# Cross-attention with an image prompt: each group's second pair of probability transfers issued by ScalarE instead of SyncE

## The chip, the core and the metric

The kernel runs on one core of a Trainium2 chip. A core has TensorE (PE, matrix products), VectorE (DVE), ScalarE (ACT), GpSimd (POOL) and SyncE (SP), each with its own instruction stream, and 16 DMA engines that move data between on-chip memory (SBUF) and device memory (HBM), and within SBUF. An engine works its instructions in the order of its stream; it waits for the others by semaphores. A transfer is an instruction in the stream of the engine that issues it; the profile shows these rows as SPq for SyncE's queue and ACTq for ScalarE's. The metric is the device time of one execution in microseconds, lower is better.

## The reference

Eight sequences (B = 8) of 112 rows and 320 channels attend to a context of 375 rows of 512 numbers, of which the last 4 are image-prompt tokens. There are 20 heads of 16 channels.

```python
q = heads(hidden_states @ W_q)
k_t = heads(text_ehs @ W_k)                    # 371 text rows
v_t = heads(text_ehs @ W_v)
probs_t = softmax(einsum('bhsd,bhtd->bhst', q, k_t) * attn_scale)
text_out = einsum('bhst,bhtd->bhsd', probs_t, v_t)
k_ip = heads(ip_ehs @ W_k_ip)                  # 4 prompt rows
v_ip = heads(ip_ehs @ W_v_ip)
attn_scores = einsum('bhsd,bhnd->bhsn', q, k_ip) * attn_scale
qsem = l2norm(einsum('bhst,bte->bhse', probs_t, text_ehs))
sem = einsum('bhse,bne->bhsn', qsem, l2norm(ip_ehs))
probs_ip = softmax(attn_scores + 0.5 * sem) * spatial_mask
ip_out = einsum('bhsn,bhnd->bhsd', probs_ip, v_ip)
out = (text_out + ip_out) @ W_out + b_out + hidden_states
```

The norm of `qsem` is computed through the Gram matrix of the context (p G p instead of the length of p times the context), so that one product of the probabilities with a table that holds the Gram matrix, the prompt's columns and the values gives everything that follows.

## The kernel before, in words

**Tiling.** The 20 heads of a batch are five groups of four. A step is one pair (b, g) of batch and group, 40 in all; the loop at L1246 works the first 35, and the last batch's five steps are written out behind it. The four heads a = 0 to 3 of a group sit in the four quadrants of 32 rows of PE.

**What a step does for its own group.** `multiplied(b, g)` (L781) sets off 48 products of the transposed probabilities `xgT` with the group's table `u` into four PSUM banks `ps_qd`, one for each head. `value_sums` (L794, ACT) copies the value columns out, `reduced` (L827, DVE) multiplies the Gram part with the probabilities and sums it; after these two the banks are free for the next step.

**What a step does for groups to come.** The scores of the group two steps ahead (LEAD = 2) are made in two pairs. `ahead(n)` names them: `now`, heads 2 and 3 of that group, at the step's start, and `then`, heads 0 and 1, of which the scores are made late in the products and the probabilities behind them. (`more` is empty but in the last two steps of the loop, where it brings in pairs of the last batch.) For a head, `scores` (L719) makes the PSUM tile `ps_s`, `probabilities` takes the maximum on DVE (L742), the exponential on ACT (L745) and, from batch 1 on, copies the four prompt logits on ACT (L747). Then `sent` (L754) moves the 112 x 371 probabilities, 162.3 KB, into the tile `xg` of a ring, 32 partitions for each head. One step before they are used, DVE transposes all of `xg` to `xgT` (L762, `transposed`), for which all four heads must have landed.

**What else stands in the queues.** SP issues nearly all transfers, in the order of the program: beside L754 the Gram tables to the groups (`u<-ug`, L553), the values to device memory and back (`vd<-vext`, L627; `vr<-vd`, L636; POOL copies them into `u` at L688), the next contexts (`ct`, L160 and L165), the next inputs (`xr_sb`, L127; `x_sb`, L1212) and the results. ACT also copies PSUM to SBUF: keys `kT` (L573 and L584), values `vext` (L618), the attention result `aT` (L987), and in the loop's last step two banks of products to `shared` (L812) for a sum that POOL and ACT take over from DVE. Between the products of two steps PE makes keys (L568, L577), values (L611), queries (L377), Gram blocks (L535) and the output of the batch before (L983, L995).

**PSUM.** `ps_qd` has four banks, `ps_sc` two for scores, `ps_mm` two for everything else. From batch 2 to 6 the last chunk of a batch's keys (L568), and the result L983 in some batches, take one of the two score banks ("spare"); the copy by ACT (L573, L987) frees it for the next scores.

**Order.** PE, SP, DVE and ACT run in the order in which the source is written (a manual schedule; POOL's is left to the scheduler within the loop). In the loop the `then` probabilities come behind `value_sums` and ahead of `reduced`, `placed` and the loads; in ACT's stream the copies of keys, values and `aT` of the stretch between two steps follow them.

Of the kernel before, what the change touches and what calls it, by code (L numbers as in the profile page):

```python
# [20 lines left out]
def kernel(  # L21
# [14 lines left out]
    nc = tc.nc  # L36
    P = 128
    B, S, C = x.shape
# [3 lines left out]
    TT = T - NIP  # L42
# [8 lines left out]
    RG = 32  # L51
# [11 lines left out]
    QN = P // RG  # L63
# [21 lines left out]
    def bank(name, spare=False):  # L85

        if spare:
            return ps_sc.tile([P, 512], F32, tag="sc", name=name)
        return ps_mm.tile([P, 512], F32, tag="mm", name=name)
# [304 lines left out]
    st = {}  # L394
# [115 lines left out]
    def gram_banks(b):  # L510

        st["ps_g", b] = ps = [bank(f"ps_g_{b}_{c}") for c in range(2)]
        for n, t in enumerate(ps):
            cleared(t, n + 1)
# [34 lines left out]
    def gram_to_groups(b, blocks, eng=nc.sync, parts=range(GROUP)):  # L549

        for q in blocks:
            for a in parts:
                eng.dma_start(  # L553
                    st[b]["u"][a * RG : (a + 1) * RG, q * GW : (q + 1) * GW],
                    ug[q * RG : (q + 1) * RG, :],
                )
# [152 lines left out]
    def scores(b, g, a, early=False, ps=None):  # L709
        s = st[b]  # L710
        _, qm, j = queries[b]
        i, r = g // 2, g % 2
        if early and (g + a // 2) % 2:

            ps = ps_qd.tile([P, 512], F32, tag="qd", name=f"ps_s_{b}_{g}_{a}")
        elif ps is None:
            ps = ps_sc.tile([P, 512], F32, tag="sc", name=f"ps_s_{b}_{g}_{a}")
        w = T if b > 0 else TT
        nc.tensor.matmul(  # L719
            ps[:S, :w],  # L720
            qm[a * RG : (a + 1) * RG, i, r, j * S : (j + 1) * S],
            s["kT"][a * RG : (a + 1) * RG, i, :w],
            start=True,
            stop=True,
        )
        s["sc", g, a] = ps

    def home(b, g):

        if b == B - 1 and g == 1:  # L730
            t = io.tile([P, NT, E], F32, tag="ct", name=f"p_{b}_{g}").rearrange("p c e -> p (c e)")
        elif b == B - 1 and g == 3:
            t = wv_sb.rearrange("p e f -> p (e f)")
        else:
            return work.tile([S, GROUP, TT], F32, tag="p", name=f"p_{b}_{g}", bufs=3)
        return t[:S, : GROUP * TT].rearrange("p (a t) -> p a t", t=TT)

    def probabilities(b, g, a, hold=False):
        s = st[b]
        ps = s.pop(("sc", g, a))  # L740
        nmx = small.tile([S, 1], F32, tag="nmx", name=f"nmx_{b}_{g}_{a}", bufs=4)
        nc.vector.tensor_reduce(nmx, ps[:S, :TT], AX.X, ALU.max, negate=True)  # L742
        if ("p", g) not in s:
            s["p", g] = home(b, g)
        nc.scalar.activation(s["p", g][:, a, :], ps[:S, :TT], AF.Exp, bias=nmx)  # L745
        if b > 0:
            nc.scalar.copy(s["ipl"][:, groups[g][a], :], ps[:S, TT:T])  # L747
        if not hold:
            sent(b, g, a)

    def sent(b, g, a):

        xg = x_ring[(b * NG + g) % NX]
        nc.sync.dma_start(xg[a * RG : a * RG + S // QN, :, :TT], st[b]["p", g][:, a, :])  # L754

    def transposed(b, g):

        xg = x_ring[(b * NG + g) % NX]
        xT = work.tile([P, BLK, P], F32, tag="xgT", name=f"xgT_{b}_{g}")
        n = BLK // 2 if b == B - 1 else BLK  # L760
        for j in range(0, BLK, n):
            nc.vector.transpose(  # L762
                xT[:, j : j + n].rearrange("p j (k q) -> p q j k", q=QN),
                xg[:, :, j * RG : (j + n) * RG].rearrange("p q (j k) -> p q j k", k=RG),
            )
        st[b]["xT", g] = xT

    def multiplied(b, g):
        s = st[b]
        xT = s.pop(("xT", g))  # L770
        banks = []
        for a in range(GROUP):

            if b == B - 1 and g % 2:
                banks.append(bank(f"ps_qd_{b}_{g}_{a}", spare=a > 1))
            else:
                banks.append(ps_qd.tile([P, 512], F32, tag="qd", name=f"ps_qd_{b}_{g}_{a}"))
        for j in range(BLK):
            c, q = PLACE[j] if b > 0 else (j // QN, j % QN)
            for a in range(GROUP):  # L780
                nc.tensor.matmul(  # L781
                    banks[a][:S, j * RG : UW],
                    xT[a * RG : (a + 1) * RG, j, :S],
                    region(b, c)[a * RG : (a + 1) * RG, q, j * RG - c * P :],
                    start=(j == 0),
                    stop=(j == BLK - 1),
                )
            yield
        s["qd", g] = banks
# [315 lines left out]
    def run(key, make, pieces=1):  # L1105

        if key not in gens:
            gens[key] = make()
        for _ in range(pieces):
            next(gens[key], None)  # L1110
# [123 lines left out]
    def ahead(n):  # L1234

        c, d = steps[n + LEAD : n + LEAD + 2]
        if steps[n] == (B - 2, NG - 2):
            todo = ((c, 2, 3), (c, 0, 1), (d, 2, 3))
        elif steps[n] == (B - 2, NG - 1):
            todo = ((c, 0, 1), (d, 2, 3), (d, 0, 1))  # L1240
        else:
            todo = ((c, 2, 3), (c,), (c, 0, 1))
        return [[(t[0], a) for a in t[1:]] for t in todo]

    ctx.enter_context(tc.manual_schedule(engines=engines | {mybir.EngineType.Activation}))
    for n, (b, g) in enumerate(steps[:-NG]):  # L1246
        now, more, then = ahead(n)
        late = (b, g) == (0, NG - 2)
        for c, a in now if not late else ():
            scores(*c, a)  # L1250
            probabilities(*c, a)
        for j, _ in enumerate(multiplied(b, g)):
            if j == 0:
                for c, a in now if late else ():
                    scores(*c, a)
                    probabilities(*c, a)
                for c, a in more:
                    scores(*c, a, ps=bank(f"ps_s_{c[0]}_{c[1]}_{a}"))
                    probabilities(*c, a, hold=True)
            if j == 6:  # L1260
                for c, a in then:
                    scores(*c, a)
            if j == 2:
                if g == 0:
                    gram_banks(b + 1)
                transposed(*steps[n + 1])
                for c, a in more:
                    sent(*c, a)
                if 1 <= g <= 3:
                    gram_to_groups(b + 1, {1: (0,), 2: (1,), 3: (3,)}[g], parts=halves[g == 2])  # L1270
                for c, i in x_loads.get((b, g), ())[: int(n > 0)]:
                    load_x_blocks(c, i)

                if g in (1, 2) and b > 0:
                    run(("f", b - 1), None)
        value_sums(b, g)
        if g == 2 and b > 0:
            run(("f", b - 1), None)
        if n == NG - 1:
            run(("t", b), lambda: prompt_logits(b))  # L1280
        for c, a in then:
            probabilities(*c, a)
        if n == len(steps) - NG - 1:
            sums = shared(b, g, GROUP // 2)
            next(sums)
            reduced(b, g, 2)
        else:
            reduced(b, g)
        placed(*steps[n + 1])
        if g == 0 and b > 1:  # L1290
            run(("f", b - 2), None)
        load_rest(n)
        if n == 0:
            load_next(2)
        if g in ctx_blocks and b < B - 3:
            load_ctx_blocks(b + 3, ctx_blocks[g])
        for c, i in x_loads.get((b, g), ())[1:]:
            load_x_blocks(c, i)
        if g == 1:
            gram_to_groups(b + 1, (0,), parts=halves[1])  # L1300
            gram_to_groups(b + 1, (1,), parts=halves[0])
        elif g == 2:
            gram_to_groups(b + 1, (2,))
        elif g == 3:
            gram_to_groups(b + 1, (3,), parts=halves[1])
            values_to_groups(b + 1)
        if g in (2, 3) and b == 0:
            run(("pp",), None)
        if (b, g) == (B - 2, 0):
            prompt_values_by_head()  # L1310
        if (b, g) == (B - 2, 1):
            bd = load_prompt_values_by_head()
        if g == 0 and b > 0:
            prompt_values(b - 1)
        between(b, g)
        if g == 1:
            values_to_dram(b + 1, nc.sync, 0, 2)
        if g == 2:
            values_to_dram(b + 1, nc.sync, 2)
# [10 lines left out]
    b = B - 1  # L1330
# [126 lines left out]
```

## Time and profile before

| what | value |
|---|---|
| median of 3 runs | 427.07 us (423.07 to 427.16) |
| the profiled execution | 426.04 us, span 424.3 us, granted clock 0.999 |
| PE busy | 415.8 us, 98% of the span |
| DVE busy | 331.5 us, 78% |
| ACT busy | 185.5 us, 44% |
| POOL busy | 111.2 us, 26% |
| DMA traffic | 65.84 MB, mean 155 GB/s |

The span is the time from the first to the last instruction that the profile records. The shares are means over the span; the digits of a slice on the page (not shown) are the same in tenths. DMA issues do not count as busy, so that SP has no share. A timeline row gives the start in us, the duration, the engine, the line, the operation with output and inputs, the number of like instructions in a row, and in brackets how long the engine sat idle ahead of it and what ended that. A scores row with "x2" is one pair of heads side by side.

### The profile page before, as it was taken

To read this page: it belongs to the slowest core of one execution; us is meant where nothing else is said; L and a number is where in the kernel's file an instruction comes from. 1 tells how busy PE (TensorE), PEld (TensorE's weight loads), DVE (VectorE), ACT (ScalarE), POOL (GpSimd) and SP (SyncE) were. 2 spreads that over 40 slices of the span, in tenths; PEclk is the share of its full clock that TensorE was granted. 3 is DMA by queue.
4 is the path that set the end of the run, shared out by engine and by line. 5 is a ranking of instruction groups with operands and counts; after the bars stand their busy time and mean duration, and the time that the engine had idled before them with its cause. 6 is when DMAs were issued, how large, how long until landed. Compare 5 with 4: busy or idle time off the path is not lost.

```text
span 424.3 us, 14021 instructions
## 1 busy us (share of the span) xinstructions
PE 415.8 (98%) x5500; PEld 327.3 (77%) x5500; DVE 331.5 (78%) x693; ACT 185.5 (44%) x647; POOL 111.2 (26%) x277
## 2 busy tenths in 40 slices
PE   8999999999998999999999999999999999999995
PEld 8867767878776977779778887788778887787993
DVE  5037668869896987889789987987898986888873
ACT  2344332335333463334533463333634363446773
POOL 6411100011160120602133220602124120515550
PEclk9999999999999999999999999999999999999999
DMA  8676846565766565666656556655555556465200
GB/s 256 184 191 198 187 122 181 155 174 152 192 157 169 141 170 154 158 175 175 169 142 167 144 158 164 159 145 158 167 151 151 134 162 181 135 167 166 66 2 29
DMA packets 61687, 65.84 MB, mean 155 GB/s; under 512 B 22072, under 2 KB 55648, under 8 KB 61622
## 3 DMA queue, kind: packets, MB, share of 16 engines
q1 hardware_dynamic: 60990, 63.98, 56.5%
q8 instruction: 44, 0.72, 0.8%
q10 hardware_dynamic: 632, 0.96, 0.7%
q14 instruction: 21, 0.17, 0.1%
HBM read 20.23 MB, written 5.32 MB: 60 GB/s over the span
## 4 chain that ended last, share of the span: by engine, by line
PE 83%; DVE 4%; ACT 3%; DMA 3%; issue 3%; SPq 2%; POOL 0%; DVEq 0%; POOLq 0%
PE ps_qd L781 34%; PE ps_v L611 14%; PE ps_k L577 10%; PE ps_s L719 9%; PE ps_g L535 7%; DMA xg<-p 2%; PE ps_q L377 2%; PE ps_o L995 2%; PE ps_g L491 1%; DVE xgT L762 1%; DVE nmx L742 1%; ACT shared L820 1%; SPq L553 1%; PE ps_w L467 1%; SPq L636 1%
## 5 line engine op out<-in xcount | busy, mean ns | idle before, releaser
L781 PE MATMUL ps_qd<-u,xgT 32*112 32x360 f32 (+11 forms) x3840 | 219.5, 351 | 1.2 <-POOL u L688 1.2
L781 PEld LDWEIGHTS ps_qd<-u,xgT 32*112 32x112 f32 x3840 | 189.1, 172 | 27.0 <-POOL u L688 2.4
L762 DVE STREAM_TRANSPOSE xgT<-xg 128x1536 f32<-128x1536 f32 (+1 forms) x45 | 119.7, 2680 | 13.9 <-DMA xg<-p 9.4
L745 ACT ACTIVATE p<-ps_s,nmx 112x371 f32<-112x371 f32 x156 | 84.9, 586 | 61.5 <-DVE nmx L742 49.3
L742 DVE TENSOR_REDUCE nmx<-ps_s 112x1 f32<-112x371 f32 x160 | 76.9, 526 | 28.3 <-PE ps_s L719 27.3
L827 DVE CUSTOM_DVE_ANT_0 junk<-ps_qd,p 112x371 f32<-112x371 f32 x146 | 79.2, 543 | 17.9 <-PE ps_qd L781 1.5
L719 PE MATMUL ps_s<-kT,qm 32*112 32x375 f32 (+1 forms) x320 | 66.7, 497 | 0.0
L688 POOL COPY u<-vr 128x64 f32<-128x64 f32 x120 | 25.7, 236 | 152.5 <-PE ps_qd L781 90.2
L611 PE MATMUL ps_v<-wv_sb,ctxT 128*128 128x384 f32 (+1 forms) x192 | 63.0, 477 | 0.0
L611 PEld LDWEIGHTS ps_v<-wv_sb,ctxT 128*128 128x128 f32 x192 | 35.7, 190 | 20.9
L794 ACT COPY pvs<-ps_qd 112x21 f32<-112x21 f32 x151 | 16.2, 189 | 74.8 <-PE ps_qd L781 74.5
L577 PE MATMUL ps_k<-ctxT,wk_sb 128*128 128x371 f32 x136 | 46.9, 488 | 0.2 <-DVE ctxT L458 0.2
L577 PEld LDWEIGHTS ps_k<-ctxT,wk_sb 128*128 128x128 f32 x136 | 24.4, 189 | 14.0 <-issue 0.5
L719 PEld LDWEIGHTS ps_s<-kT,qm 32*112 32x112 f32 x320 | 23.7, 170 | 12.6 <-issue 10.9
L535 PE MATMUL ps_g<-ctxT 128*32 128x375 f32 (+11 forms) x672 | 30.4, 333 | 0.0
L535 PEld LDWEIGHTS ps_g<-ctxT 128*32 128x32 f32 x672 | 27.7, 110 | 2.0
L618 ACT COPY vext<-ps_v 128x384 f32<-128x384 f32 (+1 forms) x24 | 11.2, 465 | 40.0 <-PE ps_v L611 39.5
L747 ACT COPY ipl<-ps_s 112x4 f32<-112x4 f32 x140 | 24.3, 174 | 0.0
L386 DVE TENSOR_SCALAR qm<-ps_q,emask 128x224 f32<-128x224 f32 (+1 forms) x25 | 9.0, 394 | 17.3 <-PE ps_q L377 17.2
L970 POOL TENSOR_TENSOR wv<-vip,w 112x1280 f32<-112x1280 f32 x6 | 14.8, 2464 | 27.7 <-DVE w L910 27.7
L437 DVE STREAM_TRANSPOSE ctxT<-ct 128x512 f32<-128x512 f32 x18 | 20.0, 1110 | 0.0
L508 POOL TENSOR_TENSOR ug<-ug,half 128x128 f32<-128x128 f32 (+1 forms) x24 | 10.4, 447 | 30.6 <-ACT ug L507 30.6
(174 smaller groups left out, 320.7 us busy)
## 6 DMA issues: line engine op xcount, KB each, us to landing
xg<-p SPq DMA_DIRECT2D x156, 162.3 KB
u<-ug SPq DMA_DIRECT2D x124, 99.0 KB
ct<-in_ctx_dram SPq DMA_DIRECT2D x24, 176.0 KB
vr<-vd SPq DMA_DIRECT2D x32, 120.0 KB
vip<-vipd SPq DMA_DIRECT2D x6, 560.0 KB
vd<-vext SPq DMA_DIRECT2D x7, 320.0 KB
vd<-vext SPq DMA_DIRECT2D x7, 160.0 KB
out_dram<-ob SPq DMA_DIRECT2D x8, 140.0 KB
```

Source lines behind the costliest of these rows:

```text
L437: nc.vector.transpose(ctxT[:, :, c * P : (c + 1) * P].rearrange("p e (j i) -> p j e i", i=RG), ct[:, some, :].rearrange("p j (k e) -> p j ...
L535: nc.tensor.matmul(ps[c][q * RG : (q + 1) * RG, j * RG - c * P : T - c * P], ctxT[:, e, j * RG : (j + 1) * RG], ctxT[:, e, j * RG : T], st ...
L577: nc.tensor.matmul(ps[:, :TT], wk_sb[:, e, i * P : (i + 1) * P], s["ctxT"][:, e, :TT], start=(e == 0), stop=(e == NE - 1),)
L611: nc.tensor.matmul(ps[:, :w], ctxT[:, e, c * P : (c + 1) * P], wv_sb[:, e, :w], start=(e == 0), stop=(e == NE - 1),)
L688: nc.gpsimd.tensor_copy(v, dealt(b, c, s["vr"][:, c * QN : (c + 1) * QN, g, :]))
L719: nc.tensor.matmul(ps[:S, :w], qm[a * RG : (a + 1) * RG, i, r, j * S : (j + 1) * S], s["kT"][a * RG : (a + 1) * RG, i, :w], start=True, st ...
L742: nc.vector.tensor_reduce(nmx, ps[:S, :TT], AX.X, ALU.max, negate=True)
L745: nc.scalar.activation(s["p", g][:, a, :], ps[:S, :TT], AF.Exp, bias=nmx)
L747: nc.scalar.copy(s["ipl"][:, groups[g][a], :], ps[:S, TT:T])
L762: nc.vector.transpose(xT[:, j : j + n].rearrange("p j (k q) -> p q j k", q=QN), xg[:, :, j * RG : (j + n) * RG].rearrange("p q (j k) -> p ...
L781: nc.tensor.matmul(banks[a][:S, j * RG : UW], xT[a * RG : (a + 1) * RG, j, :S], region(b, c)[a * RG : (a + 1) * RG, q, j * RG - c * P :], ...
L827: nc.vector.tensor_tensor_reduce(out=junk, in0=ps[:S, :TT], in1=s["p", g][:, a, :], scale=1.0, scalar=0.0, op0=ALU.mult, op1=ALU.add, accu ...
```

## The change

`sent` gets the issuing engine as an argument. For the `then` pair in the loop, `probabilities` is called with `hold=True`, so that it issues no transfer, for both heads; then both transfers are issued in ScalarE's own stream, behind the exponentials and the prompt copies of both. Before, each transfer was issued on SyncE's queue. The `now` pair, the `more` pairs, the prologue and the last batch keep SyncE.

```diff
         if not hold:
             sent(b, g, a)
 
-    def sent(b, g, a):
+    def sent(b, g, a, eng=nc.sync):
 
         xg = x_ring[(b * NG + g) % NX]
-        nc.sync.dma_start(xg[a * RG : a * RG + S // QN, :, :TT], st[b]["p", g][:, a, :])
+        eng.dma_start(xg[a * RG : a * RG + S // QN, :, :TT], st[b]["p", g][:, a, :])
...
         for c, a in then:
-            probabilities(*c, a)
+            probabilities(*c, a, hold=True)
+        for c, a in then:
+            sent(*c, a, nc.scalar)
         if n == len(steps) - NG - 1:
             sums = shared(b, g, GROUP // 2)
             next(sums)
```

In the built program 70 transfers move from SyncE's queue to ScalarE's, two in each of the 35 steps; the order on PE, DVE and POOL is the same.

## The prediction

> **What bounds the kernel.** I read the page's busy shares and its chain first, then the history of the tile `xg`, then the timelines of single steps.
>
> ```profile
> PE 415.8 (98%) x5500; PEld 327.3 (77%) x5500; DVE 331.5 (78%) x693; ACT 185.5 (44%) x647; POOL 111.2 (26%) x277
> PE 83%; DVE 4%; ACT 3%; DMA 3%; issue 3%; SPq 2%; POOL 0%; DVEq 0%; POOLq 0%
> ...
> L754 SPq DMA_DIRECT2D xg<-p x156: 800/856/1557, 26.9 to 397.8; - x156
> ...
>   DVE xgT L762: 12.1, 8
> ```
>
> TensorE (PE) is busy in 98% of the span and makes 83% of the chain that ends last. The moved transfers are 70 of the 156 rows of L754 (two in each of the 35 steps of the loop), at a median of 0.856 us: 60 us of issue leave SyncE's (SP's) queue. That is no gain by itself: DVE's transposes waited for `xg` for 12.1 us in all, and only where PE waits after them is there anything to win. So I look for the places where PE lost time, and then for those where it will.
>
> In a step PE does the two scores "now", then the value products L781, then other work (keys, values, grams). Without a stall the distance from the first score to that other work is 5.36 us (180.05 to 185.41):
>
> ```profile
> 180.05 0.57 PE L719 MATMUL ps_s<-kT,qm 32*112 32x375 f32 x2
> ...
> 185.41 1.87 PE L995 MATMUL ps_o<-wo_sb,aT 128*112 128x320 f32 x6
> ```
>
> **What the change removes from SP's path.** Three stalls of PE come from late issues on SP, all in batch 1.
>
> ```profile
> 83.28 3.26 SPq L636 DMA_DIRECT2D vr<-vd  x4
> ...
> 87.15 3.66 SPq L754 DMA_DIRECT2D xg<-p  x4
> 88.94 0.58 POOL L688 COPY u<-vr 128x64 f32<-128x64 f32 x3 [7.07 <-DMA vipd<-ipkv]
> 87.19 1.35 PE L719 MATMUL ps_s<-kT,qm 32*112 32x375 f32 x4
> 89.23 3.89 PE L781 MATMUL ps_qd<-u,xgT 32*112 32x392 f32 x54 [0.68 <-POOL u L688]
> 93.53 3.08 DVE L762 STREAM_TRANSPOSE xgT<-xg 128x1536 f32<-128x1536 f32 x1 [2.83 <-DMA xg<-p]
> 94.65 1.77 PE L535 MATMUL ps_g<-ctxT 128*32 128x375 f32 x22
> 98.92 0.57 PE L719 MATMUL ps_s<-kT,qm 32*112 32x375 f32 x2
> 104.99 5.43 PE L611 MATMUL ps_v<-wv_sb,ctxT 128*128 128x384 f32 x16
> ```
>
> - Step (1,0), that is batch 1, group 0: 87.19 to 94.65 is 7.46, so 2.1 lost. PE waited for POOL's copies, which began at 88.94, 2.4 after the issue of `vr` had ended (83.28 + 3.26 = 86.54). Two pairs of transfers fewer lie ahead of `vr` on SP; one alone is worth 2 x 0.856 = 1.7. I take 1.8 of the 2.1.
> - Step (1,1): 98.92 to 104.99 is 6.07, 0.7 lost, after a transpose that waited 2.83 for `xg`. The four sends before it ended at 90.81, and the transpose began 2.72 later: that is also my landing time for this transfer. With the pair on ScalarE (ACT) I take the 0.7 back.
> - Step (1,4):
>
> ```profile
> 127.43 1.56 SPq L553 DMA_DIRECT2D u<-ug  x2
> 129.11 1.84 SPq L754 DMA_DIRECT2D xg<-p  x2
> ...
> 133.88 2.96 DVE L762 STREAM_TRANSPOSE xgT<-xg 128x1536 f32<-128x1536 f32 x1 [2.64 <-issue]
> ...
> 137.88 0.54 PE L568 MATMUL ps_k<-ident,k 128*128 128x128 f32 x3 [1.33 <-ACT ipl L747]
> ```
>
> The pair's issue ended at 130.95, the transpose began 2.93 later, its tail held PE 1.33. SP runs late here, and loses the pair of the step before as well, so that everything comes up to 1.7 earlier; I take 1.1.
>
> Gains: 1.8 + 0.7 + 1.1 = **3.6 us**. Everywhere else the transfers were hidden by PE already. [...]
>
> **What the change puts on ACT.** Each pair now holds ACT's queue behind the second exponential and its copy L747. What is queued behind it: `kT` copies L573/L584, the aT copy L987, `vext` L618, in the last loop step the copies L812, then the next exponentials. The price of an issue by ACT:
>
> ```profile
> L553 ACTq DMA_DIRECT2D u<-ug x4: 598/604/611, 16.8 to 18.7; - x4
> L553 SPq DMA_DIRECT2D u<-ug x5: 589/597/675, 16.3 to 19.0; - x5
> ```
>
> ACT took 604 ns for a `u` where SP took 597 in the same stretch and 588 in the whole run, so I take SP's 0.87 for an `xg` (half of 1.74), 1.74 a pair. The two issued at the same time and neither got longer. [...]
>
> Second, and larger: the built program gives the DMAs of both queues eight completion semaphores in turn, in the order of its listing, and a DMA waits until the one before it on its semaphore has landed. On one queue that one is old. Now ACT's pair can be dealt a semaphore that SP used for a load of the same step, and the wait stands in ACT's queue. From the built program, step by step: nothing costly in most; in these it falls late.
>
> Step (2,4): the pair waits for the two `ct` loads, which SP issues behind what used to follow the pair.
>
> ```profile
> 186.83 1.74 SPq L754 DMA_DIRECT2D xg<-p  x2
> ...
> 189.20 0.92 SPq L160 DMA_DIRECT2D ct<-in_ctx_dram  x2
> ...
> 187.64 0.47 ACT L573 COPY kT<-ps_k 128x371 f32<-128x371 f32 x1 [0.67 <-PE ps_k L568]
> ...
> 188.68 0.57 PE L719 MATMUL ps_s<-kT,qm 32*112 32x375 f32 x2
> ```
>
> Without the pair SP reaches `ct` at 187.46, or 0.8 before that as it was already late; the first has left at 187.1 to 187.9, and lands 2.4 later (the `vr` row's 2.4), about 189.5 to 190.3. Two issues end at 191.2 to 192.0, the `kT` copy 0.5 later, and the second score needs the PSUM bank that this copy frees: at 188.8 before, at 191.7 to 192.5 after. Loss 2.9 to 3.7; I take 2.9, as SP's late start should go.
>
> Step (4,3): the pair waits for two `u` issued just ahead.
>
> ```profile
> 272.77 1.21 SPq L553 DMA_DIRECT2D u<-ug  x2
> ...
> 276.14 0.45 ACT L987 COPY aT<-ps_a 128x336 f32<-128x336 f32 x1
> ...
> 277.11 0.57 PE L719 MATMUL ps_s<-kT,qm 32*112 32x375 f32 x2
> ```
>
> First `u` away at 273.4, landed 275.4 (2.0 later) to 275.8 (2.4); pair until 277.1 to 277.5; `kT` and aT copies until 277.9 to 278.3; the second score needs aT's bank at 277.2: 0.7 to 1.1, taken 0.7. Step (6,3) is alike, with four sends between:
>
> ```profile
> 366.61 4.03 SPq L754 DMA_DIRECT2D xg<-p  x4
> ...
> 372.33 0.45 ACT L987 COPY aT<-ps_a 128x336 f32<-128x336 f32 x1
> ...
> 372.82 0.58 PE L719 MATMUL ps_s<-kT,qm 32*112 32x375 f32 x2
> ```
>
> The pair's first waits for the last of the four, landed between 373.3 (370.64 + 2.7) and 371.4 (if SP, with pairs gone from its queue, is 2 earlier); aT comes 2.6 after that, where the second score stood at 372.8: 1.2 to 3.1, taken 1.2.
>
> Step (6,4), without any wait for a semaphore:
>
> ```profile
> 380.18 0.91 ACT L812 COPY shared<-ps_qd 112x371 f32<-112x371 f32 x2
> ...
> 380.93 1.29 PE L781 MATMUL ps_qd<-u,xgT 32*112 32x392 f32 x10 [0.26 <-POOL u L688]
> ```
>
> The copies that free two banks for the third and fourth of these products move behind 1.74 of issue; they ended at 381.09, and I put PE's need of them at 0.4 after its start: 1.3, between 0.9 and 1.74.
>
> Smaller: (4,4) 0.2 (its `xr` loads land as the pair is ready), the rest of the steps with their copies 0.5. Losses: 2.9 + 0.7 + 1.2 + 1.3 + 0.2 + 0.5 = **6.8 us**.
>
> The pairs themselves lose nothing by landing later: DVE's own wait for `xg`, were it 1 us longer, is covered by PE's keys, values and grams (the 2.83 above cost PE 0.7). SP's later DMAs can wait for a semaphore of ACT's pair too, but of a pair one or more steps old, long landed: 0.
>
> **Sum.** 426.04 (the profiled execution: 424.3 span and 1.74 around it) - 3.6 + 6.8 = 429.2. The median of before is 427.07, 1.03 above that execution, so a median of after should be **430.2**.
>
> **Rivals.**
> - *Only SP's relief counts* (the other side): the semaphores' predecessors land earlier than I work out, since SP, with 60 us less to issue, runs ahead; then (2,4), (4,3), (6,3) cost 1 together and the tail little. For it: SP was behind in batch 1. Against: the `ct` of (2,4) is issued after work that needs that step's exponentials. 427.07 - 3.6 + 1 = 424.5; it decides where `ct` lands before the pair's own exponentials are done (187.0 in (2,4)), and if the early steps with no PE row of mine gain too it goes to 422.
> - *ACT's issues are longer, and every copy behind them is late.* In `xg` groups of four an issue took 4.03 / 4 = 1.0, not 0.87, and the longest was 1.56. Ten steps (all of group 4, the odd batches' group 3) have no slack between copy and second score: at 0.5 more a pair 5 us more, at 1.4 14 more: 435 to 444. It decides when an ACT row of L754 passes 0.9.
> - *Hidden either way:* PE covers both the stalls and the holds; 427.1. [...] For it: PE at 98%. Against: the PSUM banks.
> - *The change does not free the pair from SP*, since its semaphores tie it to SP's loads in 20 or so steps: gains gone but losses there, 427.07 + 6.8 = 433.9.
>
> **How the numbers follow.** Forecast (428 to 433) 0.45; SP's relief 0.18; long issues 0.15; hidden 0.10; tied 0.12. About 1% is what a measurement of this kernel can tell from no change (422.8 to 431.3). Faster: the low end of the relief, 0.08. Slower: the long issues, the tied ones and about a third of the forecast, 0.42. Within: 0.50. The range reaches from the relief's 424 to the near part of the long issues, 437.
>
> **What would show it.** ACT rows of L754, 70 of them, near 0.87; in (2,4) an ACT idle of over 2 us ahead of them, and PE's second score there waiting for L573; PE's wait for POOL at 89.23 and the 1.33 before L568 gone; SP never four `xg` in a row in batch 1; PE's products after the loop's last step waiting for L812. I am wrong if no PE wait of over 1 us stands in (2,4), or if the rows on ACT are above 1 us, or if `kT` copies hold PE in most steps.

## The result

The changed kernel takes 451.24 us (median of 6, 446.58 to 452.69), the kernel before 426.96 beside it: a ratio of 1.0563, 95% interval 1.0494 to 1.0632. It is 24 us slower; the forecast was 3 slower, and the range ended at 437.

The page of the changed kernel: busy time, the granted clock of PE in 40 slices of the span (9 is full), then the DMA queues (packets, MB, share of the 16 engines).

```profile
span 451.0 us, 13942 instructions
...
PE 428.7 (95%) x5500; PEld 337.4 (75%) x5500; DVE 331.9 (74%) x693; ACT 186.5 (41%) x647; POOL 111.6 (25%) x277
...
PEclk9999998989999999998999999999999699999999
...
q1 hardware_dynamic: 52170, 52.34, 45.2%
q10 hardware_dynamic: 9452, 12.60, 10.6%
```

DVE and ACT do the same work in the same time. PE does the same 5500 products, but is busy for 12.9 us longer and idle for 13.8 us longer (451.0 - 428.7 = 22.3, where it was 424.3 - 415.8 = 8.5). Part of why it is busier stands in the row of the granted clock, which has four slices below 9. In the kernel before it had none:

```profile
PEclk9999999999999999999999999999999999999999
```

The bytes moved are in the queue of ACT (q10) as the change says.

The history of the tile `xg`, as it was shown of before:

```profile
L754 SPq DMA_DIRECT2D xg<-p x86: 801/847/1159, 26.8 to 424.4; - x86
L754 ACTq DMA_DIRECT2D xg<-p x70: 819/822/924, 44.3 to 406.4; - x70
...
  DVE xgT L762: 17.6, 9
```

An issue by ACT costs 0.822 us in the median, and one of the 70 passes 0.9, with 0.924. The price of the issue was right, and the rival of long issues is out. What went wrong lies between the issues.

Where the time came in can be read from the start of each step's first product L781 in the two timelines. The difference after less before grows to 26.6 us, in a few places:

| between the starts of steps | grows by (us) | what stands there in the changed kernel |
|---|---|---|
| (0,2) and (0,3) | 6.5 | pairs of (0,1) and (0,2) waiting; half clock |
| (1,0) and (2,0) | 3.5 | half clock from 97.3 on; small stalls |
| (2,4) and (3,1) | 4.0 + 1.8 | pair of (2,4) waiting; half clock |
| (3,4) and (4,0) | 2.4 | pair of (3,3) waits and lands late |
| (5,4) and (6,1) | 3.7 + 1.9 | pair of (5,3) waits and lands late; half clock twice |
| (6,3) and (6,4) | 1.2 | pair of (6,3) waiting |
| (7,0) and (7,1) | 1.5 | copies L812 behind the pair of (6,4) |

The rest adds up to less than 1 us. Three mechanisms make most of these numbers, and each is shown by its rows.

**One: ACT stands in wait.** Step (2,4), timelines of SP, ACT and PE:

```profile
196.55 1.90 SPq L160 DMA_DIRECT2D ct<-in_ctx_dram  x2
...
197.16 0.17 ACT L747 COPY ipl<-ps_s 112x4 f32<-112x4 f32 x1
200.39 1.79 ACTq L754 DMA_DIRECT2D xg<-p  x2
202.22 0.47 ACT L573 COPY kT<-ps_k 128x371 f32<-128x371 f32 x1 [4.89 <-DMA xg<-p]
...
202.74 0.65 PE L719 MATMUL ps_s<-kT,qm 32*112 32x375 f32 x1 [3.04 <-ACT kT L573]
```

The pair's data are ready at 197.3, and ACT issues it at 200.39, after the two `ct` loads of SP that were dealt the same semaphores (106 and 107 in the trace) just before; the `kT` copy waits behind for 4.89, and PE for the copy for 3.04. Step (0,1) is alike, behind a `u` and a `ct` load: its first transfer begins 4.2 us after its exponential has ended. The delay runs on into (0,2); rows of ACT, DVE and PE:

```profile
61.08 1.93 ACTq L754 DMA_DIRECT2D xg<-p  x2
63.05 0.48 ACT L618 COPY vext<-ps_v 128x384 f32<-128x384 f32 x1 [5.74 <-DMA xg<-p]
...
66.45 2.96 DVE L762 STREAM_TRANSPOSE xgT<-xg 128x1536 f32<-128x1536 f32 x1 [4.48 <-DMA xg<-p]
...
71.20 1.83 ACTq L754 DMA_DIRECT2D xg<-p  x2
73.08 0.24 ACT L324 COPY kip<-ps_kip 128x96 f32<-128x96 f32 x1 [2.27 <-DMA xg<-p]
...
73.37 2.61 PE L377 MATMUL ps_q<-xT,wq_sb 128*128 128x224 f32 x6 [3.34 <-ACT kip L324]
```

**Two: the pair lands late, on top of what it waits.** Step (5,3), where the first transfer had stood in wait for 1.59 us behind `u` loads of the same step:

```profile
343.41 2.37 SPq L636 DMA_DIRECT2D vr<-vd  x4
...
343.58 1.74 ACTq L754 DMA_DIRECT2D xg<-p  x2
...
349.56 2.93 DVE L762 STREAM_TRANSPOSE xgT<-xg 128x1536 f32<-128x1536 f32 x1 [3.66 <-DMA vr<-vd]
...
353.53 0.88 PE L568 MATMUL ps_k<-ident,k 128*128 128x128 f32 x3 [2.31 <-ACT ipl L747]
```

The issue ends at 345.32, the transpose begins 4.24 later. (The bracket names `vr`, which was dealt a semaphore that one of the four `xg` had had; in the built program the transpose waits for the four `xg` alone.) The same step in the kernel before:

```profile
323.19 1.84 SPq L754 DMA_DIRECT2D xg<-p  x2
...
327.78 2.96 DVE L762 STREAM_TRANSPOSE xgT<-xg 128x1536 f32<-128x1536 f32 x1 [0.80 <-DMA xg<-p]
```

There it was 2.75. SP, free of the pair, now issues `vr` beside it, where it had issued `u` and `vr` behind it. DVE then does its later work late, and PE waits for a bank. The packets in the trace of the changed kernel show the sharing: in the nine steps in which SP's queue moved less than 15 KB beside the pair, the pair's last packet ended 1.5 to 1.6 us after its issue; in the fifteen in which SP's queue moved over 300 KB meanwhile, it ended 2.3 to 6.2 us after.

**Three: the granted clock halves after a stall.** Busy time by microsecond, PE's share first, the clock behind POOL's column:

```profile
201.00:202.00 1.00, 0.00 (x0) 0.00 (x0) 0.00 (x0) 0.00 (x0) 0.00 (x0) 1.00 0.46 94
...
204.00:205.00 1.00, 1.00 (x12) 1.00 (x8) 0.94 (x2) 0.37 (x1) 0.00 (x0) 0.50 0.28 59
205.00:206.00 1.00, 1.00 (x12) 1.00 (x8) 1.00 (x1) 0.66 (x4) 0.00 (x0) 0.50 0.34 107
```

The trace has four such stretches before the end, of 3.4, 3.4, 3.4 and 6.8 us, 17 in all; at half clock (0.50) they are worth, by an estimate, up to 17 / 2 = 8.5 of the 12.9 us by which PE is busier. (The rest stands in part in steps without half clock, 0.97 us in (2,4) and 0.94 in (3,4); no run tells what it is.) The six executions bear the clock out: the four at a mean clock of 0.98 had spans of 449.2 to 451.0 us, the two at 0.99 spans of 444.7 and 444.9. The stretches begin at 73.39, 97.28, 203.10 and 353.28 us, which are 7, 31 and 44 times 3.413 us apart; the trace's clock record gives 3.413 us for each of the first three as well, and 6.827 for the fourth. How long PE had stood before each comes below, under hold_busy. The prediction had no term for this.

### The profile page after: what moved, and what is told of

It reads as the page before. It is cut to its first block, busy times and chain, and to the rows that moved or that the text cites. A ratio compares the mean times of both kernels' runs of the same rounds, so it can differ in the third digit from the quotient of the medians.

```text
span 451.0 us, 13942 instructions
## 1 busy us (share of the span) xinstructions
PE 428.7 (95%) x5500; PEld 337.4 (75%) x5500; DVE 331.9 (74%) x693; ACT 186.5 (41%) x647; POOL 111.6 (25%) x277
## 5 line engine op out<-in xcount | busy, mean ns | idle before, releaser
L781 PE MATMUL ps_qd<-u,xgT 32*112 32x168 f32 (+11 forms) x3840 | 226.7, 358 | 0.8 <-ACT shared L812 0.6
L781 PEld LDWEIGHTS ps_qd<-u,xgT 32*112 32x112 f32 x3840 | 197.2, 175 | 25.6 <-issue 1.3
L719 PE MATMUL ps_s<-kT,qm 32*112 32x375 f32 (+1 forms) x320 | 72.6, 503 | 6.1 <-ACT kT L573 3.0
L719 PEld LDWEIGHTS ps_s<-kT,qm 32*112 32x112 f32 x320 | 26.3, 172 | 21.1 <-issue 8.0
L377 PE MATMUL ps_q<-xT,wq_sb 128*128 128x224 f32 (+1 forms) x90 | 18.8, 350 | 3.3 <-ACT kip L324 3.3
```

The source lines that it names most:

```text
L719: nc.tensor.matmul(ps[:S, :w], qm[a * RG : (a + 1) * RG, i, r, j * S : (j + 1) * S], s["kT"][a * RG : (a + 1) * RG, i, :w], start=True, st ...
L781: nc.tensor.matmul(banks[a][:S, j * RG : UW], xT[a * RG : (a + 1) * RG, j, :S], region(b, c)[a * RG : (a + 1) * RG, q, j * RG - c * P :], ...
```

## The experiments

Theory A: ACT waits for semaphores that SP's loads hold. Theory B: every issue in ACT's queue costs. Theory C: the pairs share the DMA engines with what SP now issues beside them. A line of the kernel decides for each step which queue the pair takes; unless said otherwise, each kernel is the changed one with only this line edited. A time without an interval is a single run; such kernels are read by their traces, since the kernel before itself spreads from 421.7 to 431.9 us.

**free_steps and waiting_steps: the two halves of the change.**

```diff
-            sent(*c, a, nc.scalar)
+            sent(*c, a, nc.scalar if (b, g) not in WAITING else nc.sync)
```

WAITING are (0,1), (0,2), (0,3), (1,1), (1,2), (1,3), (2,1), (2,3), (2,4), (3,3), (4,3), (4,4), (5,3), (6,3): the steps in which the pair's first transfer had waited in the changed kernel. The other kernel has `in`.

> The pair goes to ACT only in the 21 of 35 steps in which, in the changed kernel, its first transfer began within 0.1 us of its exponential; in the other 14 it stays on SP. Theory A (the loss is ACT standing in wait for a completion semaphore that SP's loads of the same step hold): no such wait, 424 to 429 us. Theory B (any issue in ACT's queue delays the copies behind it): 21 of 35 steps of 24 us, about 441. Theory C (the pairs land late because they share the DMA engines with transfers that SP now issues at the same time): a few us, 428 to 432, with late transposes.

> The complement: ACT only in the 14 steps in which the first transfer of the pair stood in wait, by 0.2 to 4.2 us. Theory A: nearly all of the 24 us, 445 to 452. Theory B: 14 of 35, about 437. Theory C: 428 to 440, by how many of the late landings lie in group 3.

Measured: free_steps 431.58 us, 1.0108 (1.0025 to 1.0192), some 4.5 us over; waiting_steps 443.26, some 16 over. 14 of the 35 steps carry about four fifths of what the two halves lose together. That is A's place, though not all of it: A's ranges, 424 to 429 and 445 to 452, are missed by 2.6 and 1.7, B's 441 and 437 by more, on both sides. Each kernel deals the semaphores anew, so that in waiting_steps two of the 14 pairs, (1,2) and (6,3), no longer wait. Something small is left in the free ones.

**only_24: the same step, other semaphores.** `nc.scalar if (b, g) == (2, 4) else nc.sync`.

> ACT in step (2,4) alone. Here the built program gives the pair the semaphores of two vr loads of the step before, long landed, where the changed kernel gave it those of two ct loads of the same step. Theory A: T0 begins within 0.1 us of its exponential, PE's second score of step (3,0) waits less than 0.5 us where it waited 3.0, no clock drop: the time of before within 1 us. Theory B: the wait of 3 us stays, +4 to +6.

Measured 427.68 us. ACT's timeline at this step:

```profile
187.05 0.63 ACT L745 ACTIVATE p<-ps_s,nmx 112x371 f32<-112x371 f32 x1
187.18 0.94 ACTq L754 DMA_DIRECT2D xg<-p  x1
...
188.23 0.86 ACTq L754 DMA_DIRECT2D xg<-p  x1
189.12 0.47 ACT L573 COPY kT<-ps_k 128x371 f32<-128x371 f32 x1 [1.40 <-PE ps_k L568]
```

The pair goes out at once, beside the second exponential. The step behind begins 0.3 us late, not 4.0. In waiting_steps, where the built program gave this pair the `ct` loads again, ACT stood 4.81 us ahead of the same copy:

```profile
198.14 1.77 ACTq L754 DMA_DIRECT2D xg<-p  x2
199.95 0.47 ACT L573 COPY kT<-ps_k 128x371 f32<-128x371 f32 x1 [4.81 <-DMA xg<-p]
```

One pair, one queue, one step; what differs at this place is the semaphores that it was dealt (two `vr` loads of the step before had them in only_24), though waiting_steps has 13 other pairs on ACT too. Theory A holds here, and B is worth at most the 0.3 at this step.

**hold_act and hold_busy: what a hold of ACT costs by itself.** No transfer is moved. In group 4 ACT makes copies that nothing uses; hold_busy also gives PE products that nothing uses, ahead of the scores at which it stood still.

```diff
+        if g == 4 and 0 < b < 6:
+            for _ in range(4 + 2 * b):
+                nc.scalar.copy(idle, p_of_the_pair)
...
+        if g == 0 and 2 < b < 7:
+            for _ in range((12, 17, 22, 28)[b - 3]):
+                nc.tensor.matmul(fill[:, :P], ident, ident, start=True, stop=True)
```

> No transfer is moved; in group 4 of batches 1 to 5, behind the exponentials of the pair, ACT makes 6, 8, 10, 12 and 14 extra copies of a 112x371 tile that nothing uses, about 0.37 us each: ACT held for 2.2, 3.0, 3.7, 4.4 and 5.2 us. If a hold of ACT alone makes the stall, PE's second score of the next step waits for the kT copy L573 by the hold less about 1.3: 1.6, 2.4, 3.1 and 3.9 us in batches 2 to 5 (batch 1 has no bank to wait for). If long stalls of PE also lower the granted clock, windows of half clock follow the longer of them and cost up to 1.7 us more each: 438 to 444 with them, 436 to 438 without.

> As hold_act, and PE makes 12, 17, 22 and 28 products of the identity, about 0.22 us each, ahead of the first scores of group 0 in batches 3 to 6, where it stood still for 2.9 to 6.7 us in hold_act. If standing still is what lowers the granted clock: no windows of half clock behind these places, and the 1.9, 1.7 and 2.5 us that hold_act lost in the steps behind them are not lost, 445 to 448 us. If the windows come from something else: 452 as in hold_act.

Measured 452.81 and 446.08 us. hold_act, batch 3: ACT (eight of the ten copies fall into the view), PE, and the clock by microsecond.

```profile
238.94 4.23 ACT L1288 COPY idle<-p 112x371 f32<-112x371 f32 x8
243.08 0.46 ACT L573 COPY kT<-ps_k 128x371 f32<-128x371 f32 x1
...
243.60 0.56 PE L719 MATMUL ps_s<-kT,qm 32*112 32x375 f32 x1 [3.03 <-ACT kT L573]
...
245.00:246.00 1.00, 1.00 (x13) 0.95 (x9) 1.00 (x2) 0.91 (x4) 0.00 (x0) 0.50 0.39 85
```

The stall of the changed kernel appears without any transfer on ACT, at the same score, 3.03 us long. The steps behind the holds of batches 2 to 5 begin 2.9, 4.0, 5.1 and 6.7 us later; the expectation had 1.6 to 3.9, and 438 to 444 us in all, since a copy takes 0.53 us (4.23 / 8) and not the 0.37 estimated. Behind the hold of batch 1, where none was expected, it is 2.5. Behind the last three of them, half clock costs 1.9, 1.7 and 2.5 more. In hold_busy, same hold, PE fills the gap (batch 6):

```profile
347.01 6.52 PE L1252 MATMUL ps_fill<-ident 128*128 128x128 f32 x56 [1.55 <-DVE ob L961]
353.46 0.57 PE L719 MATMUL ps_s<-kT,qm 32*112 32x375 f32 x2
```

Its trace has no stretch of half clock before the end, the mean clock is 0.997 against 0.985, and it is 6.7 us faster with more work on PE. Both are single runs, but the places fit: the 1.9, 1.7 and 2.5 us behind the three stalls are gone from the starts of its steps. Here standing still is what lowered the clock.

The length of a stall does not tell sharply whether half clock follows: in hold_act 1.96 had no such stretch behind it, 3.03 and more had; in the changed kernel 1.76 and 2.31 had one. It is sharper by windows. In each of the 14 traces of this document all switches of the clock lie on one grid of 3.413 us. Cut at this grid, all 11 windows at full clock in which PE stood for 1.95 us or more in sum had half clock in the window behind them; of those in which it stood for 1.64 or less none had, but for four, with 0.81 to 1.35, each the window in which step (1,0) begins. In the changed kernel the windows ahead of the four stretches had 3.34, 1.35 (step (1,0)), 3.04 and 2.06 us of standing, and the ones with 1.41 and 1.42 had no half clock behind them. The 1.96 of hold_act fell on both sides of a border, 0.81 and 1.15. So half clock came behind windows in which PE also worked (1.35 of the 3.41 us of the last of these four), and where a stall lay in the grid decided with its length. Why step (1,0) differs stays open.

**group3 and group3_vr_later: who shares the engines.** The pair on ACT in group 3 of batches 2 to 6; in the second kernel `values_to_groups(b + 1)` moves, for these, to group 4 behind the pair of heads 2 and 3.

> ACT only in group 3 of batches 2 to 6. Theory C: the transpose behind begins 3.5 to 4.3 us after the pair's issue has ended (2.3 in the kernel before), because SP issues the u and vr loads of that step at the same time instead of behind the pair; PE waits for L568 in group 4 of one to three batches, +2 to +8 us in all. Theory A (only the wait for a semaphore): a loss only where the second transfer of a pair begins over 0.5 us late, +0 to +3 us.

> The same, and the four vr loads of batches 3 to 7 are issued one step later, in group 4 behind the pair of heads 2 and 3. Theory C: the landing gets short again, 2.3 to 3 us, and PE's waits for L568 go; instead POOL's copies may wait for vr in the next step. If ACT's queue itself makes the landing long, it stays at 3.5 to 4.3.

Measured 429.3 and 436.52 us. In group3 the transposes behind the five pairs begin 2.9, 3.8, 3.8, 4.5 and 3.7 us after the pair's issue has ended, and DVE has stood still ahead of them for 0.6, 1.7, 1.0, 3.3 and 0 us; with `vr` later it is 3.0, 3.0, 3.1, 3.0 and 3.7, and 0, 0.9, 0, 0.8 and 0 us. In group3 PE waited at L568, in the other no longer, but for POOL's copies of the late `vr`, and longer. From the waits of the two:

```profile
PE ps_k L568 <- ACT ipl L747: 2.4, 2, 2.0
```

```profile
PE ps_qd L781 <- POOL u L688: 8.0, 5, 4.9
```

Theory C as far as the landing goes; the 8.0 is the price of the experiment's own edit, so that its time says nothing for or against. The semaphores dealt differ between the two as well: in group3 three of the five pairs stood in wait, by 0.5 to 1.1 us, in the other kernel none did, so that DVE's waits mix both causes. The time from the end of the issue does not.

**groups01, groups01_vip_act and sp_vip_first: the order in one queue.** groups01 has the pair on ACT in 11 steps: (0,4), group 0 of batches 1 to 6, group 1 of batches 3 to 6. groups01_vip_act issues the 560 KB load `vip` (L644) by ACT too, behind the pair. sp_vip_first leaves all on SP and issues `vip` ahead of the pair.

> ACT only in 11 steps of groups 0 and 1 (and (0,4)), in none of which the pair waited and behind which no copy is needed soon. Theories A and C: as the kernel before, 425 to 428 us, perhaps 1 less by SP's relief ahead of batch 2. Theory B (each issue in ACT's queue costs): +1.5 to +7.

> groups01, and the vip load is issued by ACT too, behind the pair in the same queue, so that the pair is again ahead of it. Theory C: the waits of 1.5 to 2.9 us for xg in group 1 fall to about those of the kernel before (0 to 0.5 us), and the time to that of the kernel before or 1 to 2 us above it. If it belongs to ACT's queue: waits and time as in groups01, 0.8% over.

> No transfer leaves SP. In group 0 SP issues the 560 KB vip load of the batch before ahead of the pair instead of behind it. Theory C (what is issued ahead of or beside the pair makes it land late): the transposes of group 1, behind these pairs, wait 1.5 to 3 us for xg, as they did in groups01, with no issue on ACT at all; time +1 to +4 us. If the late landing belongs to ACT's queue: the waits stay as in the kernel before, below 0.5 us from batch 2 on, and the time within 1 us.

Measured: groups01 429.83 us, 1.0082 (1.0038 to 1.0126); groups01_vip_act 0.9991 (0.9941 to 1.0040); sp_vip_first 423.32 in one run. The 4.0 us of groups01 lie in B's range and above what was expected of A and C, so it took the other two to tell them apart: groups01_vip_act has all eleven pairs on ACT still, and one issue more in some steps, and the loss is gone. Step (3,0) in the kernel before, SP and DVE (four `xg` in a row are the two pairs):

```profile
192.59 4.21 SPq L754 DMA_DIRECT2D xg<-p  x4
196.90 0.48 SPq L964 DMA_DIRECT2D out_dram<-ob  x1
197.44 0.41 SPq L644 DMA_DIRECT2D vip<-vipd  x1
...
200.14 3.00 DVE L762 STREAM_TRANSPOSE xgT<-xg 128x1536 f32<-128x1536 f32 x1
```

and in groups01, with ACT:

```profile
195.74 2.23 SPq L754 DMA_DIRECT2D xg<-p  x2
198.07 0.48 SPq L964 DMA_DIRECT2D out_dram<-ob  x1
198.61 0.41 SPq L644 DMA_DIRECT2D vip<-vipd  x1
...
198.22 0.85 ACTq L754 DMA_DIRECT2D xg<-p  x1
199.19 0.82 ACTq L754 DMA_DIRECT2D xg<-p  x1
...
205.34 2.96 DVE L762 STREAM_TRANSPOSE xgT<-xg 128x1536 f32<-128x1536 f32 x1 [2.54 <-DMA xg<-p]
```

On one queue the pair went ahead of the result and of `vip`, and the transpose began 3.3 us after it without waiting. On two, `vip` goes out between the pair's halves, and the transpose begins 5.3 after the pair, having waited 2.54. With `vip` behind the pair in ACT's queue:

```profile
196.10 0.82 ACTq L754 DMA_DIRECT2D xg<-p  x1
196.96 0.55 ACTq L644 DMA_DIRECT2D vip<-vipd  x1
...
199.87 2.98 DVE L762 STREAM_TRANSPOSE xgT<-xg 128x1536 f32<-128x1536 f32 x1
```

3.0 us, no wait. Over the run DVE waited for `xg` 9.4 us in 7 places before, 25.3 in 16 in groups01, and 12.5 in 10 with `vip` on ACT; the 0.8% went with it. The same lateness comes without ACT in sp_vip_first:

```profile
191.45 0.53 SPq L644 DMA_DIRECT2D vip<-vipd  x1
192.12 1.72 SPq L754 DMA_DIRECT2D xg<-p  x2
...
199.02 2.97 DVE L762 STREAM_TRANSPOSE xgT<-xg 128x1536 f32<-128x1536 f32 x1 [2.05 <-DMA xg<-p]
```

Its time is not longer, which the expectation missed: this wait PE covered. So this lateness is shown to come from the order of the transfers; what it costs depends on the slack behind. The large load in the other queue no longer waits for the pair: in groups01, from 200.0 to 202.0 us, SP's queue moved 435 KB of `vip` in 85 packets, and ACT's queue 70 KB of the pair in 47.

**sm_later and sm_vip: is a better order to be had?** The kernel before, all on SP, with `if n == 3` for the loads of mask and bias made `if n == 4`; and this together with sp_vip_first.

> The kernel before with the loads of the spatial mask and the bias (L1217, L1218) one step later, so that vr of batch 1 is issued about 1.0 us sooner on SP. If PE's stall of 2.1 us in step (1,0) hangs on SP's queue alone, 0.5 to 1.5 us less than before; if vr waits for something else there, the same.

> All transfers on SP as in the kernel before; the mask and bias loads one step later (as in sm_later) and vip ahead of the pair (as in sp_vip_first), the two orders of SP's own queue whose single profiles were shorter than that of before. If both effects are real and add: 2 to 4 us below the kernel before, interval below 1. If the single profiles only fell at the low end of the spread of before: ratio 0.995 to 1.002, not told apart.

Measured 0.9976 (0.9936 to 1.0017) and 1.0061 (1.0021 to 1.0102). In the profile of sm_later step (1,0) begins 1.9 us earlier against its neighbour than before, but in hold_act, which changes nothing there, it is 1.2 earlier too, so that one profile does not show that the stall hangs on SP's queue; and the time is not told apart from before. The two orders do not add, and sm_vip misses both of its expectations: its profile has a wait of 2.2 us at L568 and a stretch of half clock behind it. No version here beats the kernel before.

## Why the prediction was wrong

**What held.** That PE bounds; that ACT's issue costs as SP's (0.822 against 0.87); that completion semaphores dealt over both queues would stop ACT, and that (2,4) would be the worst case of batches 2 to 6; the sizes of (6,3), 1.2 forecast and 1.2 seen, of (6,4), 1.3 and 1.5, and of (4,4), 0.2 and 0.4.

**(2,4), mis-sized.** 2.9 forecast, the low end of the prediction's own 2.9 to 3.7, on the ground that SP's late start would go; 4.0 seen, then 1.8 for the clock.

**"Nothing costly in most".** Wrong for (0,1): the wait was 4.2 us, and through `vext`, the next transposes and `kip` it came to 6.5 with the clock. The prediction had put batch 0 into a sum of 0.5. Wrong too for (3,3) and (5,3), whose pairs stood in wait for 0.94 and 1.59 behind `u` loads of the same step.

**(4,3), 0.7 forecast, 0 seen.** The pair waited 0.27 only. The place of that loss was two other steps of group 3, (3,3) and (5,3), which cost 2.4 and 3.7 by another way: not the bank of `aT`, but the transpose.

**"The pairs themselves lose nothing by landing later" failed outright: 0 forecast, some 6 us seen, in part by the waits just named.** It took the wait of 2.83 that had cost PE 0.7 as the measure of every step. In group 4 PE has only L995 between the products and L568, and there the lateness arrives: 1.42 and 2.31 us at L568. And the lateness was put at 1 us, while the transposes of these two pairs began 3.9 and 4.2 us after the issue, 1.6 and 1.5 more than in the kernel before, on top of the waits for a semaphore. The prediction treated SP's 60 us as relief; what SP issued earlier is what the pair then shared the engines with (landings of 2.3 to 6.2 us beside over 300 KB of it, 1.5 to 1.6 beside under 15).

**The gains, 3.6 forecast, 0.7 seen.** Step (1,1) is 0.7 shorter, but so it is in only_24 and hold_act, which leave its transfers on SP: the prediction read this stall from one execution, and it is not there in others. Step (1,0) starts no earlier against its neighbour than it did (0.1). PE still waits at L568 for 1.41 us in (1,4), behind a pair that waited and landed late.

**The clock, no term at all.** Up to 8.5 us; up to 6.8 without the stretch at 97.3, since only_24 and group3, which leave this place as it was, have one there too.

**The rivals.** That the change does not free the pair from SP is the nearest: the semaphores tie it. Its 433.9 had the same missing terms. The rival of long issues, 435 to 444, came nearest in time, for a wrong reason: the issues are not longer.

What stays open: how the 3.5 us of batch 1 divide among clock, waits and landings, and how large the remaining loss of free_steps (4.5 us) is by cause; groups01 shows late landings for its part, (6,4) has 1.6 of it by the copies L812.

## What to carry to other kernels

One queue was also an order here: the pair of 162 KB transfers that stood ahead of the 560 KB `vip` in SP's queue lost that place when it moved to ACT's, and in step (3,0) the transpose began 5.3 us after it where it had been 3.3. Look in the built program at what each moved transfer must wait for before it is issued, and at what stands behind it in its new engine's stream: in (2,4) that wait held the `kT` copy for 4.89 us and PE for 3.04. And where TensorE is the bound, price a stall not at its length alone: in these traces all 11 windows of 3.41 us in which PE stood for 1.95 or more had half clock behind them, by an estimate up to 3.41 / 2 = 1.7 us more for each window at half clock.

## What the runs showed that was not expected

The kernel before spreads by 2% on its own (421.7 to 431.9 over all its runs), and single profiles of kernels that differ nowhere near show a short stall in step (1,0) with a stretch of half clock behind it (only_24 at 90.7 us, group3 at 89.1) or none. With ACT's pair and SP's loads at the same moment the issues do get a little longer in one place: in only_24 an `xg` took 0.94 and 0.86 where the median in the changed kernel is 0.822.
